# A fused two-layer transformer kernel: GpSimd's order in layer 0's attention, and five moves at that stage's end

## The chip, the cores and the metric

The kernel runs on one core of a Trainium2 chip. A core has five engines that run their own instruction streams and meet through semaphores: TensorE (PE, matrix products; its weight loads are shown as PEld), VectorE (DVE), ScalarE (ACT), GpSimd (POOL) and SyncE (SP), which here issues most DMAs. [...] PE writes its products into PSUM banks, from which DVE or ACT must move them before a bank is used again. The metric is the device time of one execution in microseconds.

## What is computed

Two post-norm transformer layers over x of shape (8, 512, 512), all in float32. Layer 0 is causal attention with 16 heads and a top-2 mixture of 8 experts with low-rank adapters; layer 1 is grouped attention and a feed-forward network with integer weights. Cut to what matters here, the attention and the routing of layer 0:

```python
q = (x @ WQ_w.T + WQ_b).reshape(b, s, NH, HD).transpose(0, 2, 1, 3)     # k, v alike
scores = jnp.where(causal, -jnp.inf, jnp.einsum('bhqd,bhkd->bhqk', q, k) / sqrt(HD))
out = jnp.einsum('bhqk,bhkd->bhqd', softmax(scores), v)
x = _layernorm(x + out.reshape(b, s, h) @ WO_w.T + WO_b)
probs = softmax(x @ gate_weight.T + x @ (SCALING * (gate_lora_B @ gate_lora_A)).T)
routing_weights, selected = jax.lax.top_k(probs, 2)     # then the experts, merged with their adapters
```

The softmax is done without its maximum. A guard keeps the sums and the inverses of the sums, and a general pass runs if they leave a safe range.

## The kernel before

**Tiling and units.** `attention0` handles the 8 batches (b) one after the other, each in 4 groups of 4 heads (g), each group in 3 units (u): the key blocks `UNITS = ((0,), (1, 3), (2,))` of 128 rows. I write (g,u) for a unit of a batch and (b; g,u) where the batch matters. `scores` (L1405 and on) has PE write the transposed scores sc into the one sc tile of 4 banks, ACT take their exp into p (L1420), and GpSimd set what lies above the diagonal to zero (`affine_select`, L1430: the "selects", one for each key block). One unit later `product` has PE multiply p into av (L1447) and DVE add p of the units 1 and 2 to that of unit 0 (L1455). When a group is done, `normalise` (two units later) has PE sum over keys into rs (L1462), ACT copy rs out and sum it for the guard (`watch_sums`, L1025), DVE take the reciprocal r_inv (L1465) and multiply av by it into aoT (L1466), and GpSimd add r_inv to the guard's total (`watch_inverses`, L1028).

**What goes on beside it.** `plan(b)` hangs other work on the units, in lists `todo[g, u]` (before the product) and `late[g, u]` (behind it): the values of the batch (v, L1320), the queries and keys of the next group (q, L1331 by DVE or L1329 by ACT; k, L1339), and work of the batch before: the projection ps_o with the residual (L1349), the layernorm (statistics L187 and L188 on DVE, rstd L189 and L190 on GpSimd, the scaling L192 on DVE), its transposition. For batches 0 to 5 that goes by DVE's 32x32 blocks (L95) and a DMA out (L100, "turned") and back (L103, x1T); for the last two it goes by PE (L1374). From x1T come the router's logits (L498), from these the choice of two experts (`choose`: PE's small product ps_r and some 25 small DVE instructions with one exp of ACT, L517 to L548), the place of each token (`dispatch`, ps_rank) and the table (`one_hot` by DVE, L585 to L587; `enter`, ps_table). In batches 1 to 6 each group also merges a piece of the adapters into the experts: GpSimd adds it at L805 to experts that lie in SBUF (batches 1 to 3) or at L814 to tiles that are loaded by L812 and stored by L815 (batches 4 to 6). Two such adds, i = 0 and 1, hang in `merging` on the units 1 + i after the one with u = 2. At g = 2 GpSimd adds the projection's bias to the whole x of the batch, 128x2048 (L1540).

**The end of batch 7.** Rows of the first expert tiles are gathered by GpSimd's DMAs (`first_rows`, L863) once `soon` has made their list, PE transposes three of them (`first_turned`, ps_xrT, L899), copies take them out (L900), and `begin` starts the first expert's gate and up product (ps_gu, L924; silu L925, product with up L926). Then come `tiles.step()` and the last projection in one piece per row tile (ps_o, L1343).

**What sets the order.** Before the last two groups of batch 7 a scheduler places the instructions of all engines; `in_order(tc)` there, and at the very start, keeps PE to the written order. GpSimd is left to the scheduler all through layer 0. The banks: sc has 4, av takes 2 in turn (pool `a_av`), all other products of PE share 2 in turn (`mm`).

Of the kernel before, what the change touches and what calls it, by code (L numbers as in the profile page):

```python
# [9 lines left out]
F32 = mybir.dt.float32  # L10
# [4 lines left out]
ALU = mybir.AluOpType  # L15
# [3 lines left out]
P = 128  # L19
NB = 8  # L20
S = 512
D = 512
NT = S // P
ND = D // P
# [793 lines left out]
class Tiles:  # L818
# [132 lines left out]
    def first_rows(self, room, ps):  # L951

        for i in range(3):
            self.xTs[i] = room[i].rearrange("p (c t) -> p c t", t=P)
            self.turn_rows_to(i, ps("ps_xrT").rearrange("p (c t) -> p c t", t=P),
                              self.nc.scalar.copy if i % 2 else self.nc.vector.tensor_copy)

    def begin(self, h, ps):

# [284 lines left out]
def attention0(env, guard, keep, routes, experts, dram, p_mm, tiles_ctx):  # L1244
# [4 lines left out]
    tc, nc, ins, xs, vec = env.tc, env.nc, env.ins, env.xs, env.vec  # L1249
    HD = 32  # L1250
    scale = 1.0 / math.sqrt(HD)
    UNITS = ((0,), (1, 3), (2,))
    with ExitStack() as phase:
# [5 lines left out]
        p_av = heads_ctx.enter_context(tc.tile_pool(name="a_av", bufs=2, space=PSUM))  # L1259
# [27 lines left out]
        row = work.tile([P, 2, D], F32, name="row")  # L1287
# [21 lines left out]
        def mm(shape, name):  # L1309
            return p_mm.tile(shape, F32, tag="mm", name=name)  # L1310

        def multiply(out, lhsT, rhs, c):
            matmul_by_columns(nc, out, lhsT, rhs, start=c == 0, stop=c == ND - 1)

        def value(b, t):
            ps = mm([P, D], "ps_v")
            for c in range(ND):
                multiply(ps, xts[b][:, c, ts(t, P)], wv[:, c, :], c)
            vs[t] = own.tile([P, D], F32, tag=f"v{t}", name=f"v{t}")
            nc.vector.tensor_tensor(vs[t], ps, row[:, 0, :], ALU.add)  # L1320

        def query(b, g):
            ps = mm([P, S], "ps_q")
            for c in range(ND):
                multiply(ps, wq[:, g, ts(c, P)], xts[b][:, c, :], c)
            q = own.tile([P, S], F32, tag="q", name="q", bufs=2)
            if g == ND - 1 and 0 < b <= by_blocks:

                nc.scalar.activation(q, ps, AF.Identity, bias=vec[:, V_BQ + g : V_BQ + g + 1])  # L1329
            else:  # L1330
                nc.vector.tensor_scalar(q, ps, vec[:, V_BQ + g : V_BQ + g + 1], None, ALU.add)  # L1331
            heads[b, g] = [q]

        def key(b, g):
            ps = mm([P, S], "ps_k")
            for c in range(ND):
                multiply(ps, wk[:, g, ts(c, P)], xts[b][:, c, :], c)
            k = own.tile([P, S], F32, tag="k", name="k", bufs=2)
            nc.scalar.activation(k, ps, AF.Identity, bias=vec[:, V_BK + g : V_BK + g + 1])  # L1339
            heads[b, g].append(k)  # L1340
# [4 lines left out]
        def project(b, t, out_of_heads=False):  # L1345
            ps = mm([P, D], "ps_o")
            for c in range(ND):
                (wide if out_of_heads else multiply)(ps, aoTs[b][:, c, ts(t, P)], wo[:, c, :], c)
            nc.vector.tensor_tensor(xs[b][:, t, :], ps, xs[b][:, t, :], ALU.add)  # L1349
            if t == NT - 1:  # L1350
                env.layernorm(b, router.rows[S * b : S * (b + 1)])
# [3 lines left out]
        by_blocks = NB - 2  # L1355
# [5 lines left out]
        def blocks(b):  # L1361
            room(b)
            flat = x1Ts[b].rearrange("p k s -> p (k s)")
            for t in range(NT):
                turns.blocks(flat, t, xs[b][:, t, :])
            turns.out(flat)
            turns.back(flat)
# [21 lines left out]
        def choose(b, columns=HD):  # L1389
            router.choose(b, logits.pop(b), mm([P, NT, E], "ps_r"), columns)  # L1390

        def dispatch(b, mm=mm, columns=HD):
            router.dispatch(b, mm([P, NT, E], "ps_rank"), columns)
# [63 lines left out]

        def normalise(b, g, acc):
            total, av = acc
            rs = mm([P, S], "rs")  # L1460
            for j in range(4):
                nc.tensor.matmul(rs[HD * j : HD * (j + 1), :], lhsT=ones, rhs=total[:, j, :], start=True, stop=True)  # L1462
            r_inv = work.tile([P, S], F32, tag="r_inv", name="r_inv", bufs=2)
            guard.watch_sums(rs, r_inv)
            nc.vector.reciprocal(r_inv, r_inv)  # L1465
            nc.vector.tensor_tensor(aoTs[b][:, g, :], av, r_inv, ALU.mult)  # L1466
            guard.watch_inverses(r_inv)

        merging = {}

        def plan(b):

            todo, late = ({(g, u): [] for g in range(ND) for u in range(len(UNITS))} for _ in range(2))
            for slot, places in (((0, 0), (0, 1)), ((0, 1), (3,)), ((0, 2), (2,))):
                todo[slot] += [lambda t=t: value(b, t) for t in places]
            pb, last = b - 1, b == NB - 1
            by_dma = 0 <= pb < by_blocks
            for g in range(ND):
                nb, ng = (b, g + 1) if g + 1 < ND else (b + 1, 0)
                if nb < NB:  # L1480
                    todo[g, 0 if by_dma and ng == 0 else 1].append(lambda nb=nb, ng=ng: query(nb, ng))
                    todo[g, 1 if by_dma and ng == 0 else 2].append(lambda nb=nb, ng=ng: key(nb, ng))
            if b:
                places = ((1, 0), (1, 1), (1, 2), (2, 0)) if by_dma else ((1, 0), (1, 0), (1, 1), (1, 1) if last else (1, 2))
                for t, slot in enumerate(places):
                    todo[slot].append(lambda t=t: project(pb, t))
                if by_dma:
                    todo[2, 1].append(lambda: blocks(pb))
                else:
                    for c in range(ND):  # L1490
                        at = todo[2, 1] if last and c >= 2 else (late if last else todo)[2, 0]
                        at.insert(c % 2 if at is todo[2, 1] else len(at), lambda c=c: turn(pb, c))
                todo[(3, 2) if by_dma else (2, 1)].append(lambda: score(pb))
                if not by_dma:
                    todo[2, 2].append(lambda: choose(pb))
            if b == 0:
                todo[1, 0].append(lambda: router.merge_lora(mm([P, ND, E], "ps_wr")))
            if b > 1:
                todo[0, 0].append(lambda: choose(b - 2))
                todo[1, 0].append(lambda: dispatch(b - 2))  # L1500
                todo[1, 2].append(lambda: enter(one_hot(b - 2, range(NT))))
            if last:
                todo[1, 2].append(soon)
                todo[2, 2].append(first_rows)
                late[3, 1].append(first_turned)
                todo[3, 2] += [begin, lambda: dispatch(b - 1)]
            return todo, late
# [21 lines left out]
        query(0, 0)  # L1529
        key(0, 0)  # L1530
        order = phase.enter_context(ExitStack())
        waiting = summing = None
        for b in range(NB):
            todo, late = plan(b)
            for g in range(ND):
                if g == 2:
                    if b + 1 < NB:
                        load_xT(b + 1)

                    nc.gpsimd.tensor_tensor(xs[b], xs[b], row[:, 1:2, :].to_broadcast([P, NT, D]), ALU.add)  # L1540
                if g == 3 and b + 1 < NB:
                    load_x(b + 1)
                if b == NB // 2 and g == 0:
                    experts.load_lora(work, 1)
                if b == NB - 1 and g == 1:
                    experts.load(4)
                if b == NB - 1 and g == 2:
                    order.enter_context(in_order(tc))
                if b == NB - 1 and g == 3:
                    experts.load(5)  # L1550
                    experts.load(6)
                acc = []
                for u in range(len(UNITS)):
                    p = scores(b, g, u)
                    for thunk in todo[g, u]:
                        thunk()
                    begun.close()
                    if waiting is not None:
                        waiting()
                    for thunk in late[g, u]:  # L1560
                        thunk()
                    if u == 1 and summing is not None:
                        summing()
                    waiting = lambda b=b, g=g, u=u, p=p, acc=acc: product(b, g, u, p, acc)
                summing = lambda b=b, g=g, acc=acc: normalise(b, g, acc)
# [5 lines left out]
        b = NB - 1  # L1571
# [665 lines left out]
```

## Time and profile before

| what | value |
|---|---|
| median of 3 runs | 2145.52 us (2143.09 to 2145.88) |
| the profiled execution | 2145.68 us |
| its span | 2143.9 us |
| busy: PE, PEld, DVE | 2099.9, 992.5, 1283.9 us |
| busy: ACT, POOL | 627.3, 498.1 us |
| POOL selects L1430 | 128 of 649 ns |
| POOL sums L1028 (both layers) | 64 of 1418 ns |
| POOL bias L1540 | 8 of about 4560 ns |

The busy time of an engine is that in which it executes an instruction; PE's is 98% of the span. Layer 0's attention ends at about 717 us of it, the experts fill the time to about 1100, and layer 1 the rest. The stage that is changed is thus the first third. In the list of waits a row names the engine that waits, what it wants to start, the engine and line that ended the wait, and then the us in total, the number of waits and the longest. In a timeline a row has its start and duration in us, the engine, the line, the operation, out<-in and the shapes, the count, and in brackets the idle time of the engine before it and what ended it.

### The profile page before, as it was taken

How to read it: one execution, taken by the hardware profiler on the slowest of the kernel's cores; microseconds unless marked ns; L12 is line 12 of the kernel's file. 1: busy time of each engine (PE TensorE's matmuls, PEld its weight loads, DVE VectorE, ACT ScalarE, POOL GpSimd, SP SyncE). 2: the span in 40 equal slices, each digit the busy share in tenths (PEclk: the TensorE clock that was granted, in tenths of full speed). 3: DMA queues.
4: the chain of work that ended last, by engine and by line, in shares of the span. 5: the costliest groups of instructions: out<-in, count | busy, mean ns of one | idle time of the engine just before them, and what ended most of it. 6: DMA issues, size and time to landing. Idle time of an engine off the chain costs nothing. (4 is left out here: it accounts for less than half of the span.)

```text
span 2143.9 us, 35859 instructions
## 1 busy us (share of the span) xinstructions
PE 2099.9 (98%) x15034; PEld 992.5 (46%) x15034; DVE 1283.9 (60%) x2042; ACT 627.3 (29%) x907; POOL 498.1 (23%) x489
## 2 busy tenths in 40 slices
PE   9999999999998999999999999999999999999997
PEld 2333333333333444444443333333334888888886
DVE  3557676776767634224326888888857644555443
ACT  2333333323323111121133233332332232222222
POOL 2333534434332112132024212322201000000000
PEclk9999999999999999999999999999999999999999
DMA  9020303414222338787743222231201311111000
GB/s 319 22 86 16 100 21 108 139 46 153 82 98 99 113 126 225 209 240 195 194 172 97 83 65 69 79 99 52 67 1 48 101 60 59 59 59 60 20 20 21
DMA packets 170443, 208.14 MB, mean 97 GB/s; under 512 B 61714, under 2 KB 114962, under 8 KB 167202
## 3 DMA queue, kind: packets, MB, share of 16 engines
q1 hardware_dynamic: 158992, 170.08, 25.8%
q0 software_dynamic: 10560, 34.61, 5.6%
q8 instruction: 121, 1.98, 0.4%
q10 hardware_dynamic: 722, 1.07, 0.1%
q14 instruction: 48, 0.39, 0.1%
HBM read 129.96 MB, written 75.76 MB: 96 GB/s over the span
## 5 line engine op out<-in xcount | busy, mean ns | idle before, releaser
L924 PE MATMUL ps_gu<-experts,xrT 128*128 128x512 f32 (+1 forms) x520 | 245.1, 594 | 0.0
L1420 ACT ACTIVATE p<-sc 128x2048 f32<-128x2048 f32 (+1 forms) x96 | 153.0, 1594 | 186.0 <-PE sc L62 162.4
L1028 POOL TENSOR_TENSOR g_total<-g_total,r_inv 128x512 f32<-128x512 f32 x64 | 90.7, 1418 | 489.6 <-DVE r_inv L1798 269.6
L1455 DVE TENSOR_TENSOR p<-p 128x1536 f32<-128x1536 f32 (+2 forms) x96 | 149.3, 1555 | 80.6 <-POOL p L1430 77.5
L1178 DVE SCALAR_TENSOR_TENSOR hT<-ps_u,vec,sg 128x512 f32<-128x512 f32 x88 | 65.6, 745 | 189.4 <-PE ps_u L1173 189.4
L1189 PE MATMUL ps_f<-ffn_w,h_half 128*128 128x512 f32 x672 | 169.7, 393 | 2.6 <-DVE h_half L1184 2.0
L1768 ACT ACTIVATE p<-sc 128x1024 f32<-128x1024 f32 x128 | 124.1, 1022 | 99.2 <-PE sc L62 99.2
L926 DVE TENSOR_TENSOR h<-ps_gu,h 128x256 f32<-128x256 f32 x67 | 28.4, 424 | 203.3 <-ACT h L925 203.2
L1798 DVE RECIPROCAL r_inv<-r_inv 128x512 f32<-128x512 f32 x32 | 107.1, 3346 | 67.7 <-ACT r_inv L1025 67.7
L1189 PEld LDWEIGHTS ps_f<-ffn_w,h_half 128*128 128x128 f32 x672 | 124.4, 188 | 34.7 <-DVE h_half L1184 7.6
L1173 PE MATMUL ps_g<-x_high,ffn_w 128*128 128x512 f32 x352 | 137.2, 390 | 0.8 <-DVE x L1740 0.8
L1173 PE MATMUL ps_g<-x_low,ffn_w 128*128 128x512 f32 x352 | 137.0, 389 | 0.0
L1173 PE MATMUL ps_u<-x_high,ffn_w 128*128 128x512 f32 x352 | 137.0, 389 | 0.0
L1173 PE MATMUL ps_u<-x_low,ffn_w 128*128 128x512 f32 x352 | 136.9, 389 | 0.0
L924 PEld LDWEIGHTS ps_gu<-experts,xrT 128*128 128x128 f32 x520 | 95.2, 195 | 84.4 <-issue 84.1
L940 PE MATMUL ps_y<-experts,hT 128*128 128x512 f32 (+1 forms) x272 | 127.9, 592 | 0.5 <-ACT hT L934 0.5
L62 PE MATMUL sc<-qT,kT 64*64 64x512 f32 x1024 | 124.7, 602 | 1.1 <-ACT qT L1674 0.7
L62 PE MATMUL ps_q<-experts 128*32 128x512 f32 x1024 | 120.8, 600 | 4.7 <-DMA experts<-in_xT 4.3
L62 PE MATMUL ps_v<-experts 128*32 128x512 f32 x1024 | 120.9, 594 | 0.0
L1787 PE MATMUL av<-p,v 128*64 128x512 f32 x512 | 120.8, 593 | 0.0
L1430 POOL TENSOR_SCALAR_AFFINE_SELECT p<-p 128x512 f32<-128x512 f32 x128 | 81.5, 649 | 165.3 <-ACT p L1420 158.7
L62 PE MATMUL ps_o<-attn_out,aoT 128*64 128x512 f32 x512 | 116.4, 598 | 0.8 <-ACT r_inv L1025 0.8
(270 smaller groups left out, 3254.0 us busy)
## 6 DMA issues: line engine op xcount, KB each, us to landing
results<-y SPq DMA_DIRECT2D x68, 256.0 KB, 2.4
turned<-turned SPq DMA_DIRECT2D x56, 256.0 KB, 4.1
pair<-xrT SPq DMA_DIRECT2D x25, 512.0 KB, 3.4
xrT<-pair SPq DMA_DIRECT2D x100, 128.0 KB, 4.4
x<-in_x SPq DMA_DIRECT2D x8, 1024.0 KB, 8.5
rows<-x SPq DMA_DIRECT2D x32, 256.0 KB, 2.4
x<-rows SPq DMA_DIRECT2D x8, 1024.0 KB, 16.4
experts<-in_xT SPq DMA_DIRECT2D x7, 1024.0 KB, 9.6
```

The source lines that it names most:

```text
L62: nc.tensor.matmul(out[m], lhsT=lhsT[:, m], rhs=rhs, start=start, stop=stop)
L924: nc.tensor.matmul(ps, lhsT=xT[:, c, :], rhs=self.weights(i, c), start=c == 0, stop=c == ND - 1)
L940: self.nc.tensor.matmul(ps, lhsT=hT[:, c, :], rhs=self.weights(i, ND + c), start=c == 0, stop=c == self.NI - 1)
L1028: self.nc.gpsimd.tensor_tensor(self.total, self.total, r_inv, ALU.add)
L1173: nc.tensor.matmul(ps, lhsT=w[:, ts(dc, P)], rhs=x[:, dc, :], start=(dc, i) == (0, 0), stop=(dc, i) == (ND - 1, 1))
L1189: self.nc.tensor.matmul(os[t], lhsT=h[:, ts(t, P)], rhs=self.weights(2 * NHID + c), start=(c, i) == (0, 0), stop=(c, i) == (NHID - 1, 1))
L1420: nc.scalar.activation(p, sc[:, :, :width], AF.Exp, scale=scale)
L1430: nc.gpsimd.affine_select(out=first, in_=first, pattern=[[0, 4], [1, P]], compare_op=ALU.is_ge, fill=0.0, base=0, channel_multiplier=-1)
L1455: nc.vector.tensor_tensor(total[:, :, P * kt :], total[:, :, P * kt :], p[:, :, at : at + w], ALU.add)
L1768: nc.scalar.activation(p, sc, AF.Exp, scale=scale)
L1787: nc.tensor.matmul(st["av"][HD * j : HD * (j + 1), :], lhsT=st["v"][:, kt, HD * j : HD * (j + 1)], rhs=p[:, j, :], start=kt == 0, stop=kt ...
L1798: nc.vector.reciprocal(r_inv, r_inv)
```

## The change

1. **GpSimd in written order.** In batches 1 to 6 a `manual_schedule` for GpSimd is open, so that its instructions stand in the order in which the Python issues them: in each unit the selects first, then what hangs on the unit.
2. **Bias by tiles.** In batches 1 to 6 the bias is added in four tiles of 128x512, one in the unit (g,2) of each group, instead of at once. Batches 0 and 7 keep the whole add.
3. **Sums of inverses.** In batches 0 to 6 `watch_inverses` is moved from the end of `normalise` to the unit (g+2, 0), two units later.
4. **Choice.** In batch 7 `choose(6)` moves from unit (2,2) to (3,0).
5. **First rows.** All three copies of `first_rows` go by ACT; before, two went by DVE and one by ACT.
6. **A query.** The eviction of query (7; g = 2) goes by ACT instead of DVE.
7. **The last sums.** rs of the last group of batch 7 takes a bank of av instead of one of mm.

```diff
@@ first_rows
-                              self.nc.scalar.copy if i % 2 else self.nc.vector.tensor_copy)
+                              self.nc.scalar.copy)
@@ query
-            if g == ND - 1 and 0 < b <= by_blocks:
+            if (b, g) == (NB - 1, 2) or g == ND - 1 and 0 < b <= by_blocks:
@@ normalise
-            rs = mm([P, S], "rs")
+            rs = p_av.tile([P, S], F32, tag="av", name="rs") if (b, g) == (NB - 1, ND - 1) else mm([P, S], "rs")
...
-            guard.watch_inverses(r_inv)
+            if b == NB - 1:
+                guard.watch_inverses(r_inv)
+            else:
+                merging.setdefault(len(UNITS) * (ND * b + g + 2), []).append(lambda: guard.watch_inverses(r_inv))
@@ plan
-                    todo[2, 2].append(lambda: choose(pb))
+                    todo[(3, 0) if last else (2, 2)].append(lambda: choose(pb))
@@ the loop over batches and groups
+        by_pool = phase.enter_context(ExitStack())
...
+            if b == 1:
+                by_pool.enter_context(tc.manual_schedule(engines={mybir.EngineType.Pool}))
+            if b == NB - 1:
+                by_pool.close()
...
-                    nc.gpsimd.tensor_tensor(xs[b], xs[b], row[:, 1:2, :].to_broadcast([P, NT, D]), ALU.add)
+                    if b in (0, NB - 1):
+                        nc.gpsimd.tensor_tensor(xs[b], xs[b], row[:, 1:2, :].to_broadcast([P, NT, D]), ALU.add)
+                if b not in (0, NB - 1):
+                    x = xs[b][:, g, :]
+                    merging.setdefault(len(UNITS) * (ND * b + g) + 2, []).append(
+                        lambda x=x: nc.gpsimd.tensor_tensor(x, x, row[:, 1, :], ALU.add))
```

In the built program PE's instructions stand in the same order as before but for ps_r of `choose(6)`. On GpSimd a group of batches 2 to 6 now reads: select, sum of inverses, expert add, (in group 2: rstd), two selects, expert add, select, bias tile. On SP the stores and loads of L815 and L812 alternate singly where they stood in pairs, and in batches 4 to 6 one store now stands ahead of the load of x and the return of x1T.

## Prediction

> **What bounds it now.** I read the list of waits by engine first, for TensorE (PE), from 0 to 720 us, the stretch of layer 0.
>
> ```profile
> PE   9999999999998999999999999999999999999997
> ...
> PE av L1447 <- POOL p L1430: 4.7, 5, 1.6
> PE ps_q L62 <- DMA experts<-in_xT: 4.3, 1, 4.3
> PE ps_r L62 <- DVE v L1320: 4.3, 6, 0.7
> PE sc L62 <- ACT p L1420: 2.5, 1, 2.5
> PE ps_x1T L1374 <- DVE g_routed L605: 1.6, 1, 1.6
> PE rs L1462 <- DVE first_h L926: 1.5, 1, 1.5
> PE sc L62 <- ACT k L1339: 0.8, 1, 0.8
> PE ps_o L62 <- DVE q L1331: 0.8, 1, 0.8
> ```
>
> PE is the bound, and its idle time in layer 0 is some 22 us (start included). No edit takes matmuls away, so these waits are the whole prize. Then I followed two of them through the engines' timelines, around the turn from batch 2 to 3:
>
> ```profile
> 249.94 1.07 PE L498 MATMUL ps_logits<-x1T,r_wr 128*32 128x512 f32 x8
> 252.57 1.07 PE L1447 MATMUL av<-p,v 128*32 128x384 f32 x16 [1.56 <-POOL p L1430]
> ...
> 255.46 7.07 PE L62 MATMUL ps_v<-experts 128*32 128x512 f32 x62
> 263.24 0.44 PE L62 MATMUL ps_r<-r_gather,logits 128*32 128x8 f32 x32 [0.72 <-DVE v L1320]
> ...
> 247.37 4.56 POOL L1540 TENSOR_TENSOR x<-x,row 128x2048 f32<-128x2048 f32 x1 [2.08 <-DMA x<-in_x]
> 251.86 1.24 POOL L1430 TENSOR_SCALAR_AFFINE_SELECT p<-p 128x512 f32<-128x512 f32 x2
> 258.13 1.54 POOL L1028 TENSOR_TENSOR g_total<-g_total,r_inv 128x512 f32<-128x512 f32 x1 [5.02 <-DVE r_inv L1465]
> 259.62 0.63 POOL L1430 TENSOR_SCALAR_AFFINE_SELECT p<-p 128x512 f32<-128x512 f32 x1
> ...
> 260.28 2.30 DVE L1455 TENSOR_TENSOR p<-p 128x1024 f32<-128x1024 f32 x1 [1.17 <-POOL p L1430]
> 262.50 1.28 DVE L1320 TENSOR_TENSOR v<-ps_v,row 128x512 f32<-128x512 f32 x2
> ```
>
> GpSimd (POOL) stands at fault in both. The bias of the next batch (4.56 us) lies ahead of two selects whose input was ready at 245.7, so PE waits for p. Then the sum of inverses waits for its reciprocal with a finished p behind it; VectorE's add (260.28) waits for that select, the two evictions of v wait for the add, and PE's ps_r for their bank.
>
> **Part 1: bias by tiles, GpSimd in written order.** I take from the trace the time from the start of ps_logits (8 matmuls) to the next av, in batches 1 to 6: 1.92, 2.63, 1.52, 1.17, 1.82, 2.09 us; the same 8 matmuls in batch 7, with no bias beside them, take 0.86. In the changed program the biases of batches 1 to 6 are four tiles each, behind the selects of unit (g,2), while the bias of batch 7 is still whole and still stands ahead of the selects of (6; 3,1). So five of six go: 9.06 - 5 x 0.86 = **4.76 us**. A tile should cost a quarter of 4.56, 1.14 us, up to the 1.5 of a 128x512 sum; its cover: GpSimd is 23% busy and a unit lasts some 7 us; without it a tile would cost each batch at most its 1.5 once, behind the select of (g,2), whose p nobody reads before the next unit. The expert adds also come one by one. In batches 4 to 6 they need a tile loaded by DMA (3.0 us to landing by the median, 12.3 at most); SP's new order stores and loads singly, each load a group ahead, and the add waits for no load in the trace, so 0; if one did wait, the selects behind it would.
>
> **Part 2: sums of inverses two units later.** From ps_v x62 to ps_r takes 7.78 us in each of batches 2 to 7; 64 such matmuls with no wait take 6.89, so 62 take 6.68, and 1.10 is lost each time. With the select of (3,2) right after its exp (at 251.2), VectorE's add runs at about 254.5, before v is ready, and the eviction is on time. In batch 7 the built order still has a sum ahead of that select (batch 7 is not in written order, and its thunks were hoisted), so five of six: **5.50 us**. A cross-check: from one ps_logits to the next takes 87.2, 87.9, 86.8, 86.4, 87.0 us; less the two losses of each, 85.0 every time. r_inv has two buffers, and its next writer comes four units after the moved sum: no new wait.
>
> **Part 3: query (7,2) by ScalarE (ACT).** ps_o x64 at 642.98 took 7.88 against 6.89: the eviction of q (VectorE, 646.61) stood behind the one-hots. ACT is idle from 641.6 to 652.8: **0.99 us**.
>
> **Part 4: the end of batch 7.** The rows:
>
> ```profile
> 680.00:690.00 10.00, 7.06 (x77) 0.83 0.24 100
> ...
> 682.40 1.40 PE L62 MATMUL sc<-q,k 32*64 32x384 f32 x32 [2.48 <-ACT p L1420]
> 696.70 1.06 PE L1462 MATMUL rs<-p,ones 128*32 128x512 f32 x8 [1.52 <-DVE first_h L926]
> ```
>
> With choose one unit later, ps_r stands behind the scores of (3,0), and ACT's exp of (3,0), which stood at 680.49 behind choose's small exp, runs at 679.1 to 681.0. PE's sc follows at 681.05 instead of 682.40 (1.35 earlier). The granted clock fell to 0.83 in that slice; an idle 1.57 us at 661.6 left it at 1.00, so the 1.25 that remains should too. (The Trainium skill, TensorE: Matmul & The Clock Gate, What's actually happening, puts the fall to half rate after an idle window of about 3.4 us; here 2.48 us were enough, so it gives no safe margin. By the rule no fall is to be expected either way; if it fell again, 3.4 us at half rate cost at most 1.7, of which VectorE's pace below hides 0.65.) From here VectorE sets the pace: choose resumes at 681.3 (0.7 later than now, behind ACT's exp) and ends at 685.75; it now ends at 685.0 but then stands idle 1.7 for ps_xrT and does two L900 copies (1.37) around its p add at 687.33. The three copies go to ACT (3 x 0.59, beginning after the exp of (3,1) at 684.1); PE waits about 0.9 for the first, rs(7,2) comes at 685.35 instead of 688.05. VectorE's add starts at 685.75 instead of 687.33 (1.58), one copy (0.69) and a wait (0.23) go from between it and the last aoT, one one-hot (0.2) moves ahead: the last aoT is 2.3 earlier, at 700.75. rs(7,3) in an av bank no longer waits for first_h, but for the aoT that frees that bank (693.2). PE reaches the wide ps_o at 700.1 instead of 703.61, but its third tile needs the bank that VectorE's x add (now 709.52, then about 707.0) frees, and waits 0.65. Of 3.5 us **2.85** are left at the start of the next step.
>
> **What is given back: the turned rows.** x1T goes out and back by DMA before ps_logits. Landing against need: batch 1 late (PE waited 0.5), batches 2 to 6 early by 0.6, 1.2, 0.2, 0.95, 1.0. Its chain starts at rstd:
>
> ```profile
> 311.64 0.64 POOL L1430 TENSOR_SCALAR_AFFINE_SELECT p<-p 128x512 f32<-128x512 f32 x1 [2.90 <-ACT p L1420]
> 315.54 0.23 POOL L189 TENSOR_SCALAR rstd<-mv 128x4 f32<-128x4 f32 x1 [3.26 <-DVE mv L188]
> ```
>
> The written order puts a sum (1.29) and one expert add (half of 3.50) into that idle 3.26: 3.04, no delay if neither takes longer. Behind the selects comes another expert add, beside VectorE's L192. The row: L192 x4 takes 2.53 with 1.41 us of selects beside it and 1.92 alone (720.67), so a further 1.75 us of GpSimd beside its remaining 1.1 costs 0.3 to 0.5. The Trainium skill (SBUF — State Buffer, Who interferes with whom) speaks against the change: it says that VectorE's tensor_scalar in a two-port mode and GpSimd share one port pair as an exclusive lock, and the other blocks fully; by it up to 1.75. I take 0.4 by the row. In batches 4 to 6 a store of 256 KB also moves ahead of x and x1T on SP's queue; with the DMA at 371 GB/s there, 0.7, up to 1 with its issue. Costs: batch 1 0.4, batch 4 0.8 to 0.9, batch 5 0.2, and in batch 6 the whole bias starts 0.7 later with its x. **Minus 2.1.**
>
> **Sum.** 4.76 + 5.50 + 0.99 + 2.85 - 2.1 = 12.0. The profiled execution took 2145.68 (span 2143.9 and 1.8 around it), 0.16 above the median: 2145.7 - 12.0 = **2133.7 us**. After 720 us nothing is edited, and PE stays the bound.
>
> **Rivals.**
> - *The transfer takes over.* By the full lock x1T is 1.75 late in batches 1 to 3 and 2.75 in 4 to 6; less the margins 1.75, 1.15, 0.55, 2.55, 1.8, 1.75 = 9.55, so 14.1 - 9.55 = 4.55 gained: 2141.1. For: the margins are thin, and the DMA's busy share is 0.9 to 1.0 there. Against: the measured 0.61 for the selects. 0.16.
> - *More comes back:* no transfer delay and the last bias and ps_r free too (1.23 + 1.10): 16.4, 2129.3. 0.06.
> - *Slower: rstd queues.* If the sum and the expert add ahead of rstd ran past mv, each us goes to x1T in all six batches. Summed margins are 3.95, so a delay d costs 6d - 3.95 (for d over 1.2); it passes the 14.1 from d = 3.0. With d = 4: 2145.7 - 14.1 + 20.05 = 2151.6. For: only 0.2 us is spare. Against: no GpSimd pair in the trace takes the 6 to 7 us that this needs. 0.08.
> - *It doesn't do what it says:* the scheduler's hoisting already spares batch 7's bias and sum from the new order; if VectorE, not GpSimd, also held the selects' readers in the other batches, parts 1 and 2 shrink to 2 or 3 us and part 4 is eaten by its waits: 2143. 0.04.
>
> The forecast itself: 0.66. About 0.2% (4.3 us) can be told from no change. Half of the transfer's case lies near that edge: faster 0.82, same 0.10, slower 0.08. The range is 2129.5 to 2141.
>
> **What would show it.** From one ps_logits to the next 85 to 86 us; av behind ps_logits with no wait but in batch 6; ps_r with no wait but in batch 7; a select before each sum; ps_logits waiting for x1T by up to 1 us in batches 1 and 4; clock 1.00 from 680 to 690. I am wrong if ps_logits waits for x1T by over 2 us, if rstd starts late after mv, or if the wide ps_o begins no earlier against ps_k of (7,3) than now.

## The result and the profile after

Slower by about 4 us, where 12 us faster were forecast: the median after is 2147.69 us (2144.43 to 2150.71, 22 runs), that of before beside it 2143.65 us (2140.45 to 2145.88, 22 runs); the ratio is 1.0019, 95% interval 1.0013 to 1.0024. The profiled spans are 2145.5 and 2143.9 us. In the traces the wide ps_o starts 2.78 us later than before (706.39 against 703.61); from there to the end of the span they differ by 1.1 us, in after's favour, and no edit lies there. The trace of before is of a long execution (2145.68 us, 2.0 above its median), that of after of an ordinary one (2147.35), so the traces show less of the loss than the medians.

The list of PE's waits in layer 0 (0 to 720 us), after:

```profile
PE rs L1462 <- DVE q L1331: 7.8, 5, 1.6
...
PE ps_logits L498 <- DMA x1T<-turned: 4.5, 4, 1.4
PE sc L62 <- ACT scaled L802: 2.0, 1, 2.0
...
PE av L1447 <- POOL p L1430: 1.4, 1, 1.4
```

Both waits that the change was priced on have shrunk: av for p from five times to one, and ps_r for v has no row any more. At the top stands a row that before does not have: rs for the eviction of q, five times 1.6 us. Below it x1T has grown from 0.5 us, and scaled is new.

The turn from batch 2 to 3, the same place as in the prediction, after:

```profile
250.32 1.07 PE L498 MATMUL ps_logits<-x1T,r_wr 128*32 128x512 f32 x8
251.21 1.05 PE L1447 MATMUL av<-p,v 128*32 128x384 f32 x16
...
252.20 1.27 POOL L1552 TENSOR_TENSOR x<-x,row 128x512 f32<-128x512 f32 x1
...
256.20 0.63 POOL L1430 TENSOR_SCALAR_AFFINE_SELECT p<-p 128x512 f32<-128x512 f32 x1 [2.73 <-ACT p L1420]
256.80 1.27 POOL L1028 TENSOR_TENSOR g_total<-g_total,r_inv 128x512 f32<-128x512 f32 x1
```

Here the change does what it is meant to: av follows ps_logits at once (0.89 instead of 2.63 us), the bias tile takes 1.27 us behind a select, and the sum stands behind the next select. So the loss is elsewhere. I took the time of PE's stretches from start to start in both traces; a minus is a gain:

| stretch of PE | forecast, us | measured, us |
|---|---|---|
| ps_logits to av, batches 1 to 5 | -4.76 | -4.72 |
| ps_v with ps_r, batches 2 to 6 | -5.50 | 5 x -0.90 = -4.5 |
| ps_o in front of av (7,2), for the query | -0.99 | -1.01 |
| ps_logits of batch 7 to the wide ps_o | -2.85 | 33.44 to 30.41 = -3.03 |
| sc to ps_logits (x1T), batches 1, 4, 5, 6 | +2.1, in all | 0.48 + 0.82 + 1.50 + 1.39 = +4.19 |
| turn from batch 6 to 7 | in the 2.1 | 0.42 + 2.11 + 0.13 + 0.62 = +3.28 |
| av to rs in unit (1,1), batches 2 to 6 | 0 | 1.60 + 1.69 + 1.60 + 1.70 + 1.71 = +8.30 |
| sum | -12.0 | +2.51 |

The traces differ by 2.78, so all but 0.3 us is placed. The four gains come to 13.3 us of the 14.1 that were forecast. They are given back, and more, at three places, of which the largest had no term at all.

Of the 4.0 by which the medians differ, 1.3 do not show between these two executions. The waits of before are themselves not the same in every execution: in tail_only (below), which edits nothing in batches 1 to 5, ps_logits to av takes 7.63 us in sum where the trace of before has 9.06, so part 1 is worth 1.4 us less against that execution.

**The new wait.** Timeline of before in units (1,0) and (1,1) of batch 3 (of the one-hots one is shown):

```profile
280.46 3.49 POOL L805 TENSOR_TENSOR experts<-experts,scaled 128x512 f32<-128x512 f32 x2
...
288.15 0.18 DVE L562 TENSOR_TENSOR mine<-ps_rank,r_hots 128x32 f32<-128x32 f32 x1
288.25 0.18 DVE L562 TENSOR_TENSOR mine<-r_part,r_hots 128x32 f32<-128x32 f32 x1
...
292.74 0.24 DVE L586 TENSOR_SCALAR one_hot<-r_columns,to_lane 128x128 bf16<-128x128 bf16 x1
...
296.01 0.74 DVE L1331 TENSOR_SCALAR q<-ps_q,vec 128x512 f32<-128x512 f32 x1
...
296.80 1.07 PE L1462 MATMUL rs<-p,ones 128*32 128x512 f32 x8
```

and the same place after:

```profile
285.53 1.27 POOL L805 TENSOR_TENSOR experts<-experts,scaled 128x512 f32<-128x512 f32 x1
285.88 0.18 DVE L562 TENSOR_TENSOR mine<-ps_rank,r_hots 128x32 f32<-128x32 f32 x1
285.98 0.87 DVE L562 TENSOR_TENSOR mine<-r_part,r_hots 128x32 f32<-128x32 f32 x1
...
290.10 1.33 DVE L586 TENSOR_SCALAR one_hot<-r_columns,to_lane 128x128 bf16<-128x128 bf16 x1
290.11 1.28 POOL L805 TENSOR_TENSOR experts<-experts,scaled 128x512 f32<-128x512 f32 x1
...
295.43 0.74 DVE L1331 TENSOR_SCALAR q<-ps_q,vec 128x512 f32<-128x512 f32 x1
...
296.23 1.06 PE L1462 MATMUL rs<-p,ones 128*32 128x512 f32 x8 [1.55 <-DVE q L1331]
```

VectorE runs the same chain in both: read-out of the ranks (L562), 24 one-hots (L585 to L587), then q, whose bank rs needs. Before, it ended with nothing to spare: q was out at 296.75, rs started at 296.80, 0.90 us behind its av, where an rs that waits for nothing stands 0.86 behind it. In before the scheduler had put both expert adds ahead of the chain; they were done at 283.95. The Python hangs them one and two units later, and the written order now keeps them there, beside the chain. Each stops one operation of it: the L562 takes 0.87 us instead of 0.18 and ends at 286.85, 0.05 behind the add (285.53 + 1.27); the L586 takes 1.33 instead of 0.24 and ends at 291.43, 0.04 behind the other add. From the first L562 to q it is 7.86 us before and 9.55 after: 1.69 more, and rs comes that much later behind its av (2.59 us instead of 0.90).

The L562 one row higher runs beside the same add and keeps its 0.18: it reads ps_rank from PSUM, the long one r_part from SBUF. The Trainium skill describes this case (SBUF — State Buffer, Who interferes with whom): a VectorE instruction with two inputs from SBUF contends with a GpSimd instruction that reads SBUF, a tensor_scalar in a two-port mode contends with GpSimd too, and who issues second waits until the other instruction is done. The trace agrees as to the end of the wait, to 0.05 us. In which mode the one-hots run no row shows, nor who issued first: the row of L586 starts 0.01 before that of the add.

**x1T.** The same at L192, here in batch 2; first before, then after:

```profile
229.12 2.53 DVE L192 TENSOR_SCALAR x<-x,mv,rstd 128x512 f32<-128x512 f32 x4 [1.51 <-POOL rstd L190]
```

```profile
229.42 1.41 POOL L1430 TENSOR_SCALAR_AFFINE_SELECT p<-p 128x512 f32<-128x512 f32 x2
229.49 3.50 DVE L192 TENSOR_SCALAR x<-x,mv,rstd 128x512 f32<-128x512 f32 x4 [1.51 <-POOL rstd L190]
...
230.80 1.44 POOL L805 TENSOR_TENSOR experts<-experts,scaled 128x512 f32<-128x512 f32 x1
```

The four take 3.50 us instead of 2.53; the third alone takes 1.50 instead of 0.53, and ends 0.26 behind the add. From rstd to the issue of x1T's return it is 13.9 us in before's batches 1 and 4; after, it is 14.9 in batch 1, and 15.5 in batch 4 (401.83 to 417.38), where a store also stands ahead on SP. So 1.0 us by L192 everywhere; the some 0.6 more fit the store, which was not moved alone.

**The turn from batch 6 to 7**, where batch 7's bias is still whole:

```profile
598.86 4.53 POOL L1548 TENSOR_TENSOR x<-x,row 128x2048 f32<-128x2048 f32 x1 [3.91 <-DMA x<-in_x]
...
603.34 1.22 POOL L1430 TENSOR_SCALAR_AFFINE_SELECT p<-p 128x512 f32<-128x512 f32 x2
604.01 2.16 DVE L1455 TENSOR_TENSOR p<-p 128x1536 f32<-128x1536 f32 x1 [10.77 <-POOL p L1430]
...
604.53 2.77 POOL L814 TENSOR_TENSOR merged<-merged,scaled 128x512 f32<-128x512 f32 x1
...
607.33 0.60 ACT L802 ACTIVATE scaled<-sc 128x512 f32<-128x512 f32 x1 [5.51 <-POOL merged L814]
...
607.98 1.25 PE L62 MATMUL sc<-q,k 32*64 32x512 f32 x16 [2.04 <-ACT scaled L802]
609.16 8.15 PE L62 MATMUL ps_v<-experts 128*32 128x512 f32 x59
...
609.00:612.00 3.00, 3.00 (x24) 0.50 0.32 89
```

The bias waits for its load, then holds up the selects: their p is out of ACT at 601.33, and they start only where the bias ends. The selects hold up the expert add that now stands behind them, the add holds up the tile `scaled` that ACT is to write next, and that the bank of PE's next scores. The last two links are new: before has no wait of PE for `scaled` in layer 0.

The last row is of PE alone from 609 to 612 us, and the number behind the count is the granted clock: 0.50. PE has stood idle for 1.45 and 2.04 us shortly before, and its clock is halved for some 3.4 us, which neither before nor the other turns of after show. The 59 products of ps_v take 8.15 us, and ps_v with ps_r 8.67, where the five turns before it take 7.15. So the 3.28 us of this row in the table are 0.42 (av) and 2.11 (scaled), 1.65 by the halved clock (1.52 here, 0.13 in the sc before), less the 0.90 that part 2 gains here as in the other batches.

### The profile page after: what moved, and what is told of

Read it like the earlier page. It is cut to its first block, busy times and chain, and to the rows that moved or that the text cites. A ratio compares the mean times of both kernels' runs of the same rounds, so it can differ in the third digit from the quotient of the medians.

```text
span 2145.5 us, 35932 instructions
## 1 busy us (share of the span) xinstructions
PE 2097.9 (98%) x15034; PEld 994.4 (46%) x15034; DVE 1273.3 (59%) x2039; ACT 629.9 (29%) x910; POOL 490.9 (23%) x507
## 5 line engine op out<-in xcount | busy, mean ns | idle before, releaser
L1455 DVE TENSOR_TENSOR p<-p 128x1536 f32<-128x1536 f32 (+2 forms) x96 | 121.8, 1269 | 41.4 <-PE av L1447 28.9
```

The costliest lines, as they stand in the source:

```text
L1455: nc.vector.tensor_tensor(total[:, :, P * kt :], total[:, :, P * kt :], p[:, :, at : at + w], ALU.add)
```

## The experiments

Each was run beside the kernel before on the same chip. Times in us:

| kernel | median | before beside it | ratio, 95% interval |
|---|---|---|---|
| pool_only | 2151.20 | 2142.73 | 1.0038, 1.0025 to 1.0052 |
| tail_only | 2139.37 | 2142.73 | 0.9986, 0.9979 to 0.9992 |
| adds_at_once | 2133.07 | 2142.73 | 0.9957, 0.9943 to 0.9970 |
| q_by_act | 2140.27 | 2142.73 | 0.9986, 0.9980 to 0.9993 |
| late0 | 2134.52 | 2143.15 | 0.9956, 0.9943 to 0.9969 |
| late1 | 2146.32 | 2143.15 | 1.0012, 1.0006 to 1.0019 |
| both | 2135.59 | 2143.15 | 0.9957, 0.9944 to 0.9970 |
| all3 | 2131.38 | 2143.15 | 0.9948, 0.9935 to 0.9960 |
| both4 | 2130.32 | 2143.09 | 0.9938, 0.9924 to 0.9951 |
| adds_again | 2132.79 | 2143.09 | 0.9947, 0.9934 to 0.9961 |
| bias7 | 2145.85 | 2143.09 | 1.0011, 1.0003 to 1.0019 |
| load1_sooner | 2151.56 | 2143.09 | 1.0036, 1.0023 to 1.0050 |

### Which half loses: pool_only, tail_only

pool_only is before with the hunks of `watch_inverses` and of the loop over batches and groups (the change's parts 1 to 3); tail_only is before with the other four:

```diff
-            if g == ND - 1 and 0 < b <= by_blocks:
+            if (b, g) == (NB - 1, 2) or g == ND - 1 and 0 < b <= by_blocks:
...
-                    todo[2, 2].append(lambda: choose(pb))
+                    todo[(3, 0) if last else (2, 2)].append(lambda: choose(pb))
```

> The kernel before with GpSimd's part alone (written order, bias by tiles, sums two units later); the query, choose, first rows and the bank of the sums at the end of batch 7 are left as before. Theory A (the loss is made in batches 2 to 6 by GpSimd's new order, and the edits at the end of batch 7 work as forecast): about 6.5 to 7 us slower than before (the 5.81 us by which ps_logits of batch 7 comes later in the changed kernel, and the 0.99 us of the query); PE's rs waits for q five times by about 1.6 us; the end of batch 7 as before. Rival B (the edits at the end of batch 7 cost time that the comparison hides): no slower than before, or faster.

> The kernel before with the four edits at the end of batch 7 alone (query by ScalarE, choose one unit later, first-row copies by ScalarE, the last sums in an av bank); GpSimd as before. Theory A: 3.5 to 4 us faster than before (0.99 for the query, 2.85 for the end), to about 2139.7 to 2140.2; the wide ps_o some 3.9 us earlier; no rs waits for q in batches 2 to 6. Rival B: within 1 us of before.

GpSimd's half alone loses 8.5 us, the end's half alone gains 3.4. Their sum, 5.1, is near the change's 4.0. The rs waits of pool_only are those of after (7.8 us, five times). Its median is 1.5 us above the expected; in its profile the first 48 us, where nothing is edited, took 1.2 more than after's. tail_only has no rs wait for q. So the loss is in GpSimd's half.

### The place of the adds: adds_at_once

Both adds go back to the unit of their scaled product, behind the bias tile; selects, sums and bias stay as changed.

```diff
-            return {1 + i: lambda: nc.gpsimd.tensor_tensor(w, w, scaled, ALU.add)}
+            return {0: lambda: nc.gpsimd.tensor_tensor(w, w, scaled, ALU.add)}
...
-        return {i: load, 1 + i: lambda: nc.gpsimd.tensor_tensor(w[0], w[0], scaled, ALU.add),
-                2 + i: lambda: nc.sync.dma_start(out=self.merged[:, e : e + 2, f], in_=w[0])}
+        w = self.ahead.pop(i)
+        return {0: lambda: nc.gpsimd.tensor_tensor(w, w, scaled, ALU.add),
+                1: lambda: nc.sync.dma_start(out=self.merged[:, e : e + 2, f], in_=w)}
...
+            if u == 1 and NB // 2 <= b < NB - 1:
+                for i in range(2):
+                    experts.load_pair(i, ND * (b - 1) + g, own)
```

> The changed kernel with both expert adds of a unit (g,2) run in that unit again, right behind its bias tile, as the kernel before has them; the load of the merged tiles is issued one group earlier and their store one unit later, so that SP has no store ahead of x and x1T. Selects, sums and bias stay in the changed order. Theory A (the moved adds lengthen VectorE's one-hot operations, and q's eviction behind them comes late): one-hot operations of 0.2 to 0.3 us where they now take 0.9 to 1.3, rs without a wait for q in batches 2 to 6 (8 us back), PE waits less for x1T in batches 4 to 6 (1 to 3 us back): 2135 to 2139, 8 to 12 us faster than the changed kernel. Rival B (it is PE's earlier arrival, or the selects and sums beside the one-hots, that make q late): rs still waits 1.2 us or more in each of the five batches, and the time stays above 2144.

9.7 us faster than before, and so some 14 us faster than the changed kernel. Its timeline at the place shown above (lines shifted: q is L1334, rs L1468):

```profile
283.81 0.18 DVE L562 TENSOR_TENSOR mine<-r_part,r_hots 128x32 f32<-128x32 f32 x1
...
288.30 0.24 DVE L586 TENSOR_SCALAR one_hot<-r_columns,to_lane 128x128 bf16<-128x128 bf16 x1
...
291.56 0.74 DVE L1334 TENSOR_SCALAR q<-ps_q,vec 128x512 f32<-128x512 f32 x1
...
292.36 1.06 PE L1468 MATMUL rs<-p,ones 128*32 128x512 f32 x8
```

The chain has its old lengths (7.85 us from the first L562 to q) and rs stands 0.88 to 0.99 us behind its av in the five batches, as in before, although PE comes here earlier than in any kernel so far; that refutes rival B. L192 x4 is back at 2.53. From one ps_logits to the next it is 85.2 us from batch 1 to 5 and 85.3 from 5 to 6, where before took 86.4 to 87.8; the forecast's cross-check had 85.0. The gain exceeds the upper end expected (12), because the turn to batch 7 gets shorter too: 70.8 us from ps_logits of batch 6 to that of batch 7, instead of 74.5, with the clock at 1.00.

### The wait, taken away at its other end: q_by_act

```diff
-            if (b, g) == (NB - 1, 2) or g == ND - 1 and 0 < b <= by_blocks:
+            if g == 2 and b > 1 or g == ND - 1 and 0 < b <= by_blocks:
```

> The changed kernel with the eviction of the query of group 2 by ScalarE in batches 2 to 6 as it is in batch 7, so that it stands behind no one-hot operation; GpSimd and its adds unchanged. Theory A: the one-hot operations stay as long as in the changed kernel, but rs waits no more for q: 6.5 to 8.5 us faster than the changed kernel, 2139 to 2141. Rival B (the whole chain of VectorE is late, and k's bank or v's eviction behind the one-hots becomes the wait in q's place): under 3 us faster, with a new wait of 1 us or more at the next query, k or v.

2.5 us faster than before, so 6.5 faster than the changed kernel. From av to rs it is 0.86 us in all five batches, and the L562 still takes 0.86. So what costs is not the longer chain as such, but q's place at its end. Not all of the 8.3 comes through: in batches 1 to 6 PE waits 6.4 us before ps_logits, for x1T, scaled and p, where it waited 4.5. The clock falls to 0.50 at the turn to batch 7 here too.

### One add at a time: late0, late1

adds_at_once, with one of the two adds put back where the change has it (j = 0 or 1):

```diff
-            return {0: lambda: nc.gpsimd.tensor_tensor(w, w, scaled, ALU.add)}
+            return {1 + i if i == j else 0: lambda: nc.gpsimd.tensor_tensor(w, w, scaled, ALU.add)}
...
+        if i == j:
+            w = []
+            return {i: lambda: w.append(self.load_pair(i, k, own)),
+                    1 + i: lambda: nc.gpsimd.tensor_tensor(w[0], w[0], scaled, ALU.add),
+                    2 + i: lambda: nc.sync.dma_start(out=self.merged[:, e : e + 2, f], in_=w[0])}
```

> As adds_at_once, but the first of the two expert adds runs one unit late again, in unit (1,0), beside VectorE's read-out of the ranks (L562); the second stays at once. Theory A (each add that runs beside VectorE's chain lengthens one operation of it by the rest of the add, and q's eviction and rs follow one for one): the L562 from r_part takes 0.85 to 0.9 us instead of 0.18, no one-hot over 0.8; rs waits 0.55 to 0.75 us in each of batches 2 to 6; L192's four operations keep their 2.77 us; 3 to 4 us slower than adds_at_once, 2136 to 2137. Rival B (only both adds together make q late): within 1 us of adds_at_once.

> As adds_at_once, but the second of the two expert adds runs two units late again, in unit (1,1) behind its selects, beside VectorE's one-hot operations; the first stays at once. Theory A: a one-hot operation of 1.2 to 1.4 us instead of 0.25, the L562 at 0.18; rs waits 0.9 to 1.1 us in each of batches 2 to 6; L192's third operation takes 1.5 us instead of 0.53 in batches 1 to 6, and x1T is 1 us later; 5 to 7 us slower than adds_at_once, 2138 to 2140. late0 and late1 together give back what the changed kernel's rs waits (1.7 us each). Rival B (only both adds together make q late): within 1 us of adds_at_once.

late0, then late1, in batch 3:

```profile
284.54 1.27 POOL L806 TENSOR_TENSOR experts<-experts,scaled 128x512 f32<-128x512 f32 x1
...
285.00 0.87 DVE L562 TENSOR_TENSOR mine<-r_part,r_hots 128x32 f32<-128x32 f32 x1
...
294.15 1.06 PE L1473 MATMUL rs<-p,ones 128*32 128x512 f32 x8 [0.46 <-DVE q L1340]
```

```profile
290.81 1.37 DVE L587 TENSOR_SCALAR one_hot<-r_columns,r_to_column 128x256 bf16<-128x256 bf16 x1
290.81 1.28 POOL L806 TENSOR_TENSOR experts<-experts,scaled 128x512 f32<-128x512 f32 x1
...
296.39 1.07 PE L1473 MATMUL rs<-p,ones 128*32 128x512 f32 x8 [1.05 <-DVE q L1340]
```

Another one-hot is stopped in late1, and it too ends 0.09 behind the add. From av to rs it is 0.9 us with both adds at once, 1.5 with the first late, 1.9 to 2.1 with the second late, 2.6 with both: the two shares, 0.5 to 0.6 and 1.0 to 1.2, add up to the whole, 1.6 to 1.7. L192 has 2.77 us (the sum of its four) in late0 and 3.74 in late1, so it is the second add that lies beside it. The times were not met as well. late0's layer 0 is 3.35 us later at the last av than that of adds_at_once, but its median only 1.5: the layer that follows gave the rest back (1449.8 us from the last av to the end in adds_at_once, 1448.2 in late0). late1 loses 13 us to adds_at_once, twice what was expected; its waits tell where: x1T 2.9 us, and scaled 4.9 us in four waits. An add alone behind the two selects of (1,1) keeps the second `scaled` busy, and one of these adds also waits 5.8 us for its own load.

### The load: load1_sooner

```diff
-        return {i: load, 1 + i: lambda: nc.gpsimd.tensor_tensor(w[0], w[0], scaled, ALU.add),
-                2 + i: lambda: nc.sync.dma_start(out=self.merged[:, e : e + 2, f], in_=w[0])}
+        return {0: load, 1 + i: add} if i else {0: load, 1: add, 2: store}
```

(`add` issues the store too where i is 1.)

> The changed kernel with the load of the second pair of merged tiles one unit sooner on SP's queue, ahead of x and x1T instead of behind x1T and the next inputs, and its store right behind its add; the adds stay where the change has them. Theory (the loss lies in the adds' place beside VectorE, and the late load is a small further part): GpSimd's waits of 4.5 and 5.2 us for that load gone, and with them PE's 2.0 us for scaled in batch 6; PE waits for x1T by 0.5 to 1 us more in batches 4 to 6, as 256 KB more lie ahead of it; rs waits 1.7 us five times as before; 2145 to 2149. Rival (the late load is the main cause): rs no longer waits, and 5 us or more faster than the changed kernel.

In after, two adds of batches 4 and 5 wait 4.5 and 5.2 us for this load, which the forecast had put at none. Here these waits are gone, rs waits 7.7 us as before, and the time is some 4 us worse than that of the changed kernel: PE still waits 5.1 us for x1T and 2.5 for scaled, and from batch 3's ps_logits to batch 4's it is 89.2 us instead of 87.7. In after, PE waits for x1T beside it, and av follows with no wait, so the late load cost nothing there. It is not the main cause: in batches 2 and 3, whose adds load and store nothing, rs comes as late (1.60 and 1.69 us) as in batches 4 to 6. The median missed the expected range by 2.6 us; which of the shifted DMAs costs this was not followed.

### The bias of batch 7: bias7, both, both4

bias7 and both divide it like this, on the changed kernel and on adds_at_once; both4 takes `range(NT) if g == 0 else ()` in place of the pairs.

```diff
+                if (b, g) == (NB - 1, 2):
+                    by_pool.close()
...
-                if b not in (0, NB - 1):
-                    x = xs[b][:, g, :]
+                for t in () if b == 0 else (g,) if b < NB - 1 else (2 * g, 2 * g + 1) if g < 2 else ():
+                    x = xs[b][:, t, :]
```

> The changed kernel with the bias of batch 7 by tiles (two in (7;0,2), two in (7;1,2)) and the sums of (7,0) and (7,1) two units later; the expert adds as in the changed kernel. Theory: av behind ps_logits of batch 6 without a wait (1.65 us), the wait for scaled of 2.0 us smaller or gone, ps_r of batch 7 without a wait (0.7 us), against up to 1 us lost at L192 of batch 6; the five rs waits of 1.7 us stay: 1.5 to 3.5 us faster than the changed kernel, 2144 to 2146. Rival (the bias of batch 7 has no part in the loss): within 1 us of the changed kernel.

> adds_at_once, and the bias of batch 7 by tiles too, two in each of the units (7;0,2) and (7;1,2), with GpSimd's written order kept until group 2 of batch 7 and the sums of (7,0) and (7,1) two units later. Theory (the whole bias of batch 7 ahead of the selects is what is left at the turn from batch 6 to 7): ps_logits of batch 6 to av 0.86 us instead of 1.77, the ps_r of batch 7 without a wait; 1.5 to 2.5 us faster than adds_at_once, 2130.5 to 2131.6. Rival (two tiles of bias in one unit reach into the next selects): no faster than adds_at_once.

> both, with all four bias tiles of batch 7 in unit (7;0,2), where GpSimd stands idle for 7 us behind them, and none in (7;1,2), where two of them ran beside L192 and lengthened its third operation to 1.5 us. Theory: L192 of batch 6 back to 3.0 us, ps_x1T of the end about 1 us earlier than in both, ps_logits of batch 7 at 658.8 to 659.3 instead of 659.84; 0.5 to 1 us of layer 0 gained against adds_at_once, which is near what the times can tell: 2131 to 2133. Rival (g_routed sets that point whatever L192 takes): ps_logits of batch 7 at 659.8 again.

bias7: from ps_logits of batch 6 to that of batch 7 it is 71.5 us instead of 74.5, the 3 us that were expected. The av wait, the scaled wait and the halved clock are gone from the turn (5.4 us), and ps_v with ps_r is back at 7.15. In return, in batch 7, PE's ps_x1T waits 2.5 us instead of 1.6, and the clock falls to 0.50 behind that wait. The median shows 1 to 2 of the 3 us, and the profile none: ps_logits of batch 1 came 2.1 us late there, and the stretches to batch 6 took 1.4 more.

both missed what was expected: its median, 2135.59, is no better than that of adds_at_once. av and ps_r at the turn wait no more, and yet that stretch is 71.3 us, where adds_at_once takes 70.8 and, run once more, 71.4. What was gained at the turn is lost behind it:

```profile
643.69 2.71 POOL L1558 TENSOR_TENSOR x<-x,row 128x512 f32<-128x512 f32 x2
644.83 3.74 DVE L192 TENSOR_SCALAR x<-x,mv,rstd 128x512 f32<-128x512 f32 x4
...
651.56 1.09 PE L1377 MATMUL ps_x1T<-ident,x 128*128 128x128 f32 x8 [2.54 <-DVE g_routed L605]
652.58 1.97 PE L62 MATMUL sc<-q,k 32*64 32x384 f32 x32
...
652.70:656.00 3.30, 3.30 (x39) 0.50 0.01 2
```

Two of the tiles run beside L192, which takes 3.74 us instead of 2.78, and PE's ps_x1T waits 2.5 us for VectorE instead of 1.6. It is the loss of the changed kernel once more, made by my own edit. Behind that wait the granted clock falls to 0.50 (last row, PE alone): the 32 products of sc take 1.97 us where both4 and all3 take 1.12, and from sc to ps_logits it is 7.26 us instead of 5.95, 1.3 more. both4 puts these tiles where GpSimd stands idle:

```profile
645.47 2.78 DVE L192 TENSOR_SCALAR x<-x,mv,rstd 128x512 f32<-128x512 f32 x4
```

and that stretch is 69.1 us, 2.3 less than in both: 1.0 by the shorter wait and 1.3 by the clock, which stays at 1.00. The longest of layer 0's waits of both4:

```profile
PE ps_q L62 <- DMA experts<-in_xT: 4.6, 1, 4.6
PE ps_x1T L1377 <- DVE g_routed L605: 1.6, 1, 1.6
PE rs L1468 <- DVE aoT L1472: 1.4, 1, 1.4
PE sc L62 <- ACT p L1423: 1.2, 1, 1.2
```

In the whole list neither av, ps_r nor rs for q is found. both4 is the fastest version: 2130.32 us, 12.8 below before, ratio 0.9938.

### all3 and adds_again

all3 is both with the edit of q_by_act; adds_again is adds_at_once once more.

> both, and the query of group 2 evicted by ScalarE in batches 2 to 6. Since rs no longer waits for q once the adds are out of the way, theory A expects nothing from it: within 1 us of both. Rival (q is still the narrowest point of each batch): 1.5 us or more faster than both.

> adds_at_once once more, beside both4 on the same chip: 2132 to 2134, as before; av of the end of batch 7 at 681 to 682 us. It shows how far two runs of one kernel differ in the layer that follows, where nothing is edited.

The median of all3 lies 4.2 us below that of both, where at most 1 us was expected. Its last av comes only 0.5 us earlier (680.80 against 681.31), though its first 48 us took 1.2 longer. From ps_logits of batch 1 to that of batch 7 it takes 1.7 us less; 1.3 of that is the halved clock of both, which all3 does not have, and 0.4 is left for the query. The other 3.9 lie in the next layer (below). So the query by ACT brings next to nothing once the adds are gone from beside the one-hots, but the medians alone would not have shown it. adds_again repeats adds_at_once to 0.3 us.

## Why the prediction was wrong

**What failed** is a step of part 1: "The expert adds also come one by one." I priced these moved adds at rs by their loads alone ("the add waits for no load in the trace, so 0"), and never asked what VectorE does beside the ranks and one-hots at their new place. They cost 8.3 us at rs. Traces and runs agree on it: undone, the wait is gone (adds_at_once); each add alone gives its share (late0, late1); with q led past the chain, rs stands free though the chain is as long (q_by_act).

**A size that was off, from the same cause:** in "What is given back" the second add beside L192. I weighed the row (0.3 to 0.5, from selects) against the lock of the Trainium skill (SBUF — State Buffer, Who interferes with whom; up to 1.75) and took 0.4. It measured 0.97: the wait was full, for what was left of the add. Selects of 0.63 us had made a row that looks like a mild slowing; they are short, so what is left of one is short too. Had I applied the rule to every two-port or two-input VectorE operation that the moved adds of 1.27 us meet, the chain of one-hots would have been charged with up to 2.5 us a batch. The trace of before shows no slack against it: rs already came right behind q. The forecast would then have been about no change.

**The turn to batch 7** I put into those 2.1 us as a bias that starts 0.7 later. It cost 3.3 net. An add behind the selects now also holds `scaled`, and behind the two waits the clock fell, which I had considered only at the end of batch 7. bias7 agrees: 3.0 us of that stretch come back, although the clock falls there at a later place.

**Part 2** was 0.2 us too high per batch (0.90, not 1.10), since the stretch in which ps_r and the last products of ps_v now alternate keeps 0.2 us; why was not followed. In batch 7, where I had kept the wait of ps_r, it is gone too.

**Right:** part 1's bias tiles (4.72 for 4.76), part 3 (1.01 for 0.99), and part 4 (3.03 for 2.85), with the granted clock back at full speed at the place where before shows 0.83:

```profile
680.00:690.00 10.00, 8.81 (x148) 3.45 (x140) 8.76 (x24) 4.98 (x6) 2.79 (x3) 1.00 0.73 276
```

(the column behind the five engines is the clock). And of the rivals: rstd never queued behind the sum and the add (it waits for mv, 0.79 us before 228.08), so the slower case fell with its mechanism, although its sign came true. "The transfer takes over" came true in part: 4.2 of its 9.55 us. None of the three signs by which I would have known to be wrong came: the longest wait for x1T is 1.4 us, rstd is on time, and the wide ps_o came 3.0 us earlier behind ps_k of (7,3). The loss lay where I had set no sign.

With both4 the four gains stand and what was given back is nearly gone: 12.8 us. That this is near the forecast's 12.0 is chance, as both4 also divides the bias of batch 7 and moves two of its sums; adds_at_once, nearer to the change that was forecast, has 9.7. The gains were read rightly for the trace at hand; the list of what they would push aside was not complete.

## What to carry to other kernels

When an edit puts one engine into a fixed order, list every instruction that this moves, not only those it is about, and for each the work that it will lie beside. For GpSimd that means: a VectorE operation beside one of its instructions may wait out the whole rest of it (0.7 us at L562, 1.1 at L586, 1.0 at L192), so keep GpSimd's long ones away from chains of small VectorE operations, or lead what PE waits for past that chain. A reader that starts 0.05 us behind the end of a chain waits for it already; look for such ends before pricing anything beside them at nothing. And add up what a wait of PE does to its clock: look at the granted clock in small windows, not over the whole span, whose mean is 0.997 and 0.998 for after and before.

## What was not expected of the hardware

- Whether VectorE waits for GpSimd is decided operand by operand: beside the same add an L562 with one input from PSUM kept 0.18 us, and the next, with both from SBUF, took 0.87.
- The other way round GpSimd waits as well: an expert add takes 1.27 us alone and 2.77 beside VectorE's add of p, which reads two tiles of SBUF (604.01 and 604.53, above).
- The clock is halved after short waits, and not after each: to 0.50 for some 3.4 us after an idle 2.48 us (before, 683 us), after 1.45 and 2.04 (after, 609 us) and after 2.54 (both, 653 us), but not after 2.53 at the same place in all3, nor after 1.27 and 2.04 in late1. All are shorter than the 3.4 us that part 4 of the prediction quotes. What decides between 2.54 and 2.53 stays open.
- The time from the last av of layer 0 to the end of the span is 1448.1 to 1449.8 us in 13 of the 14 profiles, and 1452.5 in one (both). There PE stands 2.3 us at the start of layer 1 (to 1103.35) with no releaser shown, and behind it the clock is 0.50 again: the next 16 products take 3.57 us, and 16 such take 1.95 a little later, so stop and clock are 3.9 us, and without them it would be 1448.6. The first 48 us of layer 0 differ by up to 1.7. A difference of 1 to 3 us between two medians here is thus read only with the stretches of the trace beside it. What makes the stop and the other differences stays open.
